# Three of seven skip products per batch summed in the states' PSUM banks, and other GpSimd costs for the planner

## Chip, cores, metric

One core of a Trainium2 chip runs the program. The metric is the device time of one execution in microseconds (us). Three runs of the kernel before took 464.29, 464.99 and 465.58 us, median 464.99.

## What is computed

Four sequences of 1024 tokens, 256 features each, float32. Four layers follow one another, each added to its input, each on a layer normalization of it: causal attention; a gated feed-forward (sigmoid gate, squared ReLU, each token mixed with its predecessor); a state-space layer; the same feed-forward again. The change is in the third, which cut to what matters is:

```python
xz = layernorm(x) @ W_in.T + b_in
x_proj, z = split(xz); z = silu(z)
B_proj = x_proj @ W_B.T * dt.mean()
x_mean = causal convolution of B_proj over time, one decay kernel per state (16 states)
y = (x_mean @ W_C.T + D_skip * x_proj) * z      # states' share + skip, gated
x = x + y @ W_out.T + b_out
```

## The kernel before

**Tiles.** A sequence ("batch" b, four of them) is two halves j = 2b and 2b+1 of 512 tokens. For the products of the third layer the normalized input lies turned, features on the partitions: xnT[j] is 128 x 2 x 512 (two blocks of 128 features). A product of one 128 x 128 weight block with one 128 x 512 data block fills one PSUM bank; in the profile it is two 128x512 matmul instructions[...]. PSUM is held as four single "banks" (pool ps_bank) and two "pairs" of banks (ps_pair).

**Seven products for eight.** The skip share of a batch is a 2 x 2 block product: output blocks (e, h), feature block e and half h. seven_products (L821) makes it with seven instead of eight products from sums of weight blocks (x_sums, weight_sums L789) and sums of data blocks (T1 to T4, stream_sums L796). Each product p1 to p7 takes a bank (unit, L826); VectorE then adds it from PSUM onto running sums (add, L834; with a bias by L840, without by L838), p1 is copied into a scratch u (ScalarE or VectorE, copies L761). The same routine makes the gates z (gates_of_batch L1680, weights wz), the queries and the second feed-forward's keys (keys_of_batch L974, tiles *_gks). skips_of_batch (L1866) calls it for the skips of batches 1 to 3; batch 0 has a plain form (skip L1841, mix_states L1920). All are generators that give one product per step, and more_gates(n) takes the next n steps of one long chain: for b = 1, 2, 3 the seven gate products of b, then the seven skip products of b.

**States' share.** mix_states_apart(b) (L1880) makes four products with contraction over 16 states only, one per quarter of TensorE's rows, which run abreast, each to a bank of its own in two pairs py (L1889). VectorE adds each to the skip block (grown, L1899), then z is multiplied by that (gated, L1903, GpSimd or VectorE). The states come by DMA (states_out, states_in L1829: tile xmT) after the convolution (L1798). Then state_outputs (L1949) multiplies with W_out (pr_pyo) and VectorE adds the result to x (L1956), and mix2.prepare normalizes it for the next layer: statistics, a power on GpSimd (L642), tiles rs_g, mrs_g, xn_g; a turn through DRAM (hT_g, L731); mixing with the predecessor (xk_g, xr_g, L927 and L930); gates r_g (L1016), values (pr_g.pv), gating (L1038), adding to x on GpSimd (L1044) and storing.

**Order of the work.** TensorE's order is written out by hand: the sequence of o.unit calls at the end of hybrid_kernel (scores, more_gates(8), mix_states(0) and so on). Each engine runs its own queue in order, so a waiting instruction holds all behind it. The orders of the other engines are made while the program is built, by the planner Order (L53). Each operation states what it needs and one or more ways, (engine, cost in us, emitter); _way (L248) takes the way that would end first by these costs. Due times are counted backwards from the products that need a result (_backwards, L131). "POOL" is GpSimd; "DVE+port" marks a VectorE operation that the planner never lets run together with GpSimd's (_start, L257). It makes 20 plans with 5 rounds each (finish, L178) and emits the one that ends first by its own costs. So a changed cost can move any operation that is planned, in all layers. A sum T or a gating z has two ways: GpSimd at 1.05, or VectorE at dve(512) = 0.62 with the port.

Of the kernel before, what the change touches and what calls it, by code (L numbers as in the profile page):

```python
# [15 lines left out]
ALU = mybir.AluOpType  # L16
# [13 lines left out]
HALF = 512  # L30
# [310 lines left out]
def dve(n):  # L341
    return 0.02 + n / 850
# [7 lines left out]
def hybrid_kernel(  # L350
# [55 lines left out]
    def pair(name):  # L406
        return ps_pair.tile([P, 2 * HALF], F32, tag="pair", name=name)
# [7 lines left out]
    def lazy(make):  # L415
        box = []

        def get():
            if not box:
                box.append(make())  # L420
            return box[0]

        return get
# [372 lines left out]
    def stream_sums(key, src, needs):  # L796

        t = [lazy(lambda k=k: cols(f"T{k}_{key}")) for k in range(KC)]

        def b(c, h):  # L800
            return src(h)[:, c, :]

        def sums(k):
            return t[(k - 1) // 2]()[:, (k - 1) % 2, :]

        for k, plus, minus in (
            (1, lambda: b(0, 1), lambda: b(0, 0)),
            (3, lambda: b(1, 1), lambda: b(0, 1)),
            (2, lambda: b(1, 1), lambda: sums(1)),
            (4, lambda: b(1, 0), lambda: sums(2)),  # L810
        ):
            def emit(engine, k=k, plus=plus, minus=minus):
                engine.tensor_sub(sums(k), plus(), minus())

            o.op(
                f"{key}.T{k}", needs + ([f"{key}.T{k - 1}"] if k in (2, 4) else []),
                ("POOL", 1.05, partial(emit, nc.gpsimd)), ("DVE+port", dve(HALF), partial(emit, nc.vector)),
            )
        return sums

# [78 lines left out]
    class Mix:  # L899
# [4 lines left out]
        def prepare(self, j, by_hand=False):  # L904

            b, h = divmod(j, 2)
            key = f"{self.tag}{j}"
            hT = self.hT[j] = lazy(lambda: cols(f"hT_{key}", HALF + 1))
            xk = self.xk[j] = lazy(lambda: cols(f"xk_{key}"))
            xr = self.xr[j] = lazy(lambda: cols(f"xr_{key}"))  # L910
            names = [f"{key}.hT{c}" for c in range(KC)]
            self.rows[j] = normalized(
                key, b, h, self.needs(j), lambda c: hT()[:, c, 1:], names, by_hand=by_hand,
                by_scalar=self.last and j < BY_SCALAR,
            )
            if h == 0:
                first = lambda: nc.gpsimd.memset(hT()[:, :, 0:1], 0.0)
                before = [f"{key}.xn0"]
            else:
                old = self.hT[j - 1]  # L920
                first = lambda: nc.gpsimd.tensor_copy(hT()[:, :, 0:1], old()[:, :, HALF:])
                before = [f"{self.tag}{j - 1}.hT{c}" for c in range(KC)] + [f"{key}.xn0"]
            o.op(f"{key}.h", before, ("POOL", 0.2, first))
            for name, t, mu, mu1 in (("xk", xk, muk, muk1), ("xr", xr, mur, mur1)):
                for c in range(KC):
                    def scale(t=t, mu=mu, c=c):
                        nc.scalar.mul(t()[:, c, :], hT()[:, c, 1:], mu[:, c : c + 1])  # L927

                    def add(t=t, mu1=mu1, c=c):
                        nc.vector.scalar_tensor_tensor(  # L930
                            t()[:, c, :], hT()[:, c, :HALF], mu1[:, c : c + 1], t()[:, c, :],
                            ALU.mult, ALU.add,
                        )

                    o.op(
                        f"{key}.{name}m{c}", [names[c], "mu1"],
                        ("ACT", act(HALF), scale),
                        delay=0.0 if name == "xk" else 0.8,
                    )
                    o.op(  # L940
                        f"{key}.{name}{c}", [f"{key}.{name}m{c}", f"{key}.h"],
                        ("DVE+port", dve(HALF) + 0.06, add),
                    )
# [77 lines left out]
        def values(self, j, g):  # L1021
            b, h = divmod(j, 2)
            key = f"{self.tag}{j}"
            r, last = self.r[j], self.last
            if last and j == 2 * NB - 1:
                for n in range(2 * g, 2 * g + 2):
                    for d0, d1 in ((0, P), (P, D)) if n == NH - 1 else ((0, D),):
                        self.last_values(j, n, d0, d1)
                return
            pv = project_rows(  # L1030
                f"{key}.pv{g}", w_fv, self.ka[j], g,
                [f"{key}.ka{c}" for c in range(KC)] + ["w_fv"],
            )
            n0 = h * NH + 2 * g

            def gate():
                rg = r()[:, ts(g, 2), :]
                nc.vector.scalar_tensor_tensor(rg, rg, 1.0, pv(), ALU.add, ALU.mult)  # L1038

            dst = out[b].rearrange("(n p) d -> p n d", p=P)  # L1040

            def add():
                xg = x[b][:, n0 : n0 + 2, :]
                nc.gpsimd.tensor_add(xg, xg, r()[:, ts(g, 2), :])  # L1044

            def store():
                nc.sync.dma_start(dst[:, n0 : n0 + 2, :], x[b][:, n0 : n0 + 2, :])

            o.op(
                f"{key}.rv{g}", [f"{key}.g{g}", f"{key}.pv{g}"], ("DVE", dve(HALF), gate),  # L1050
                frees="bank",
            )
            o.op(f"{key}.x{g}", [f"{key}.rv{g}"], ("POOL", 1.27, add))
            if last:
                o.op(None, [f"{key}.x{g}"], ("SP", 0.47, store), moves=[move(8 * P * D, 1024, True)])

# [616 lines left out]
    def sums_of_batch(b):  # L1673
        if b < NB and b not in T_of:
            T_of[b] = stream_sums(
                f"zs{b}", lambda h: xnT[2 * b + h](), columns_of(2 * b) + columns_of(2 * b + 1)
            )
        return T_of.get(b)
# [187 lines left out]
    def skips_of_batch(b):  # L1866

        there = columns_of(2 * b) + columns_of(2 * b + 1)
        src = lambda h, xb=(xnT[2 * b], xnT[2 * b + 1]): xb[h]()
        for j in (2 * b, 2 * b + 1):  # L1870
            skips[j] = lazy(lambda j=j: cols(f"skip_{j}"))
        sb = [skips[2 * b], skips[2 * b + 1]]
        sums_of_batch(b + 1)
        yield from seven_products(
            f"ss{b}", f"zs{b}", wx_block, lambda k: x_sums[:, k - 1, :], src, sums_of_batch(b),
            lambda e, h: sb[h]()[:, e, :], lambda e: b_skip[:, e : e + 1],
            ["x_sums", "b_all"], there,
        )

    def mix_states_apart(b):  # L1880

        for h in range(2):
            py[2 * b + h] = lazy(lambda h=h: pair(f"py_{2 * b + h}"))

        def emit():
            for e in range(KC):
                for h in range(2):
                    k = 2 * e + h
                    nc.tensor.matmul(  # L1889
                        py[2 * b + h]()[:, ts(e, HALF)],  # L1890
                        lhsT=w_c[k * GRP : k * GRP + S, ts(e, P)],
                        rhs=xmT[b]()[k * GRP : k * GRP + S, ts(h, HALF)],
                        start=True,
                        stop=True,
                    )

        def grown(j, e):
            t = skips[j]()[:, e, :]
            nc.vector.tensor_add(t, py[j]()[:, ts(e, HALF)], t)  # L1899

        def gated(engine, j, e):
            t = z[j]()[:, e, :]
            engine.tensor_mul(t, t, skips[j]()[:, e, :])  # L1903

        o.unit(f"pm{b}", 1.0, ["w_c", f"xmT{b}"], emit, "pair", many=2)
        for h in range(2):
            j = 2 * b + h
            for e in range(KC):
                o.op(
                    f"g{e}.{j}", [f"pm{b}", f"ss{b}.c{e + 1}{h + 1}"],  # L1910
                    ("DVE", dve(HALF) + 0.03, partial(grown, j, e)),
                    frees="pair" if e else None,
                )
                o.op(
                    f"y{e}.{j}", [f"g{e}.{j}", f"z{e}.{j}"],
                    ("POOL", 1.05, partial(gated, nc.gpsimd, j, e)),
                    ("DVE+port", dve(HALF), partial(gated, nc.vector, j, e)),
                )

# [207 lines left out]
    for b in range(NB):  # L2127
        states_in(b)
    skip(1)
    more_gates(8)  # L2130
    mix_states(0)
    more_gates(8)
    outputs(0)
    more_gates(5)
    mix_states_apart(1)
    outputs(1)
    more_gates(4)
    outputs(2)
    more_gates(4)
    mix_states_apart(2)  # L2140
    outputs(3)
    more_gates(3)
# [86 lines left out]
```

## Time and profile before

| What | Value |
|---|---|
| median of three runs | 464.99 us |
| the profiled execution | 465.0 us |
| its span, first to last instruction | 463.1 us |
| granted TensorE clock | 1.000 |
| T sums of batches: VectorE, clean (T_gks) | 0.684 us each |
| the same on GpSimd (T_gks) | 1.27 to 1.47 us each |
| gating z, GpSimd | 9 at 1.46 us |
| gating z, VectorE | 3 at 0.744 us |
| adding to x, GpSimd (L1044, second feed-forward) | 14 at 1.37 us |
| state products (L1889) | 8 instructions in 1.07 us |

How to read it: the span is cut into instructions of five engines that run side by side, each in its own order: PE (TensorE's matmuls; PEld its weight loads), DVE (VectorE), ACT (ScalarE), POOL (GpSimd), SP (issues DMAs). A row of the timeline has start, length, engine, line, operation, output<-inputs, and in brackets the idle time before and who ended it. A length holds the time in which an instruction waits inside its engine, so the same small operation can be 0.15 us in one place and 1.2 in another; and successive instructions of one engine overlap by some 0.08 us, so the distance from start to start is what a queue pays. A row of the view of waits has the waiting engine and tile, the releaser, the idle us in total, how often, and the longest.

### The profile page before, as it was taken

How to read it: one execution, taken by the hardware profiler on the slowest of the kernel's cores; microseconds unless marked ns; L12 is line 12 of the kernel's file. 1: busy time of each engine (PE TensorE's matmuls, PEld its weight loads, DVE VectorE, ACT ScalarE, POOL GpSimd, SP SyncE). 2: the span in 40 equal slices, each digit the busy share in tenths (PEclk: the TensorE clock that was granted, in tenths of full speed). 3: DMA queues.
4: the chain of work that ended last, by engine and by line, in shares of the span. 5: the costliest groups of instructions: out<-in, count | busy, mean ns of one | idle time of the engine just before them, and what ended most of it. 6: DMA issues, size and time to landing. Idle time of an engine off the chain costs nothing.

```text
span 463.1 us, 6634 instructions
## 1 busy us (share of the span) xinstructions
PE 456.0 (98%) x2052; PEld 312.5 (67%) x2052; DVE 390.2 (84%) x931; ACT 220.8 (48%) x463; POOL 143.1 (31%) x149
## 2 busy tenths in 40 slices
PE   8999999999999999999999999999999999999996
PEld 5766785667786667786777775474565758675875
DVE  3687769899969999889999977459889999999962
ACT  3422414454342433333556567441458777664652
POOL 3000102112013213121271354962052616826340
PEclk9999999999999999999999999999999999999999
DMA  8047876848455763427866989603022024252442
GB/s 242 21 127 203 250 190 168 222 132 258 117 135 139 221 194 93 118 62 237 224 177 182 275 268 271 260 17 88 11 92 91 1 86 144 81 147 99 129 144 84
DMA packets 84915, 69.44 MB, mean 150 GB/s; under 512 B 20160, under 2 KB 82576, under 8 KB 84880
## 3 DMA queue, kind: packets, MB, share of 16 engines
q1 hardware_dynamic: 84064, 68.76, 50.8%
q10 hardware_dynamic: 816, 0.26, 0.2%
q8 instruction: 16, 0.26, 0.2%
q14 instruction: 19, 0.16, 0.1%
HBM read 40.54 MB, written 28.45 MB: 149 GB/s over the span
## 4 chain that ended last, share of the span: by engine, by line
PE 86%; DVE 8%; issue 2%; DMA 1%; POOL 1%; ACT 1%; SPq 0%; DVEq 0%; POOLq 0%
PE po L1597 13%; PE sc L1492 13%; PE pv L1464 5%; PE p_zs L830 4%; PE p_ss L830 4%; PE p_qs L830 2%; PE p_gks L830 2%; PE py L1848 2%; PE pc L1798 2%; PE dust L1282 1%; DMA blocks_a<-rows_a 1%; PE pr_g0.pr L881 1%; PE pb L1735 1%; PE pp_a0.pq L774 1%; PE pr_g0.pv L881 1%
## 5 line engine op out<-in xcount | busy, mean ns | idle before, releaser
L1597 PE MATMUL po<-v,prT 128*128 128x256 f32 x288 | 67.7, 380 | 0.1
L1492 PE MATMUL sc<-xa,q 128*128 128x512 f32 (+3 forms) x192 | 67.0, 486 | 0.0
L1597 PEld LDWEIGHTS po<-v,prT 128*128 128x128 f32 x288 | 54.2, 189 | 11.6 <-issue 2.6
L1513 ACT ACTIVATE pr<-pr,nmx 128x128 f32<-128x128 f32 (+7 forms) x32 | 24.7, 773 | 64.6 <-DVE pr L1508 57.7
L1492 PEld LDWEIGHTS sc<-xa,q 128*128 128x128 f32 x192 | 35.1, 190 | 24.5 <-issue 19.6
L1464 PE MATMUL pv<-wv,xa 128*128 128x257 f32 x128 | 32.9, 380 | 0.0
L642 POOL TENSOR_TENSOR rs_a<-ve_a,minus_half 128x4 f32<-128x4 f32 x7 | 7.1, 1010 | 76.8 <-DVE ve_a L629 76.8
L1044 POOL TENSOR_TENSOR x<-x,r_f 128x512 f32<-128x512 f32 x16 | 20.3, 1271 | 33.0 <-DVE r_f L1038 32.5
L642 POOL TENSOR_TENSOR rs_h<-ve_h,minus_half 128x8 f32<-128x8 f32 x8 | 13.2, 1647 | 52.5 <-DVE ve_h L631 52.5
L1464 PEld LDWEIGHTS pv<-wv,xa 128*128 128x128 f32 x128 | 23.6, 191 | 7.8 <-issue 3.6
L1508 DVE TENSOR_SCALAR_CACHE_REDUCE pr<-sc,v 128x128 f32<-128x128 f32 (+7 forms) x32 | 26.2, 818 | 1.1
L1550 DVE STREAM_TRANSPOSE prT<-pblocks 128x384 f32<-128x384 f32 (+7 forms) x30 | 23.8, 793 | 2.4 <-DMA pblocks<-exps 2.3
L642 POOL TENSOR_TENSOR rs_f<-ve_f,minus_half 128x4 f32<-128x4 f32 x8 | 8.4, 1053 | 47.1 <-DVE ve_f L629 28.8
L1044 POOL TENSOR_TENSOR x<-x,r_g 128x512 f32<-128x512 f32 x14 | 18.9, 1371 | 11.0 <-DVE r_g L1038 11.0
L1641 POOL TENSOR_TENSOR x<-x,bout_r 128x512 f32<-128x512 f32 x16 | 20.0, 1279 | 4.5 <-ACT x L1634 4.5
L1606 DVE SCALAR_TENSOR_TENSOR x<-po,rsm,x 128x256 f32<-128x256 f32 x32 | 15.0, 470 | 4.3 <-PE po L1597 3.8
L1474 DVE TENSOR_TENSOR v<-pv,bv_r 128x257 f32<-128x257 f32 x32 | 13.4, 418 | 5.6 <-PE pv L1464 5.6
L930 DVE SCALAR_TENSOR_TENSOR xr_g<-hT_g,mur,xr_g 128x512 f32<-128x512 f32 x16 | 17.3, 1112 | 0.0
L663 ACT ACTIVATE xn_f<-x,mrs_f,rs_f 128x256 f32<-128x256 f32 x18 | 9.8, 592 | 15.5 <-DVE mrs_f L651 15.5
L1634 ACT ACTIVATE x<-x,mrs_h,rs 128x256 f32<-128x256 f32 x32 | 16.9, 592 | 0.0
L1903 POOL TENSOR_TENSOR z<-z,skip 128x512 f32<-128x512 f32 x9 | 13.1, 1462 | 10.9 <-DVE skip L1899 10.7
L663 ACT ACTIVATE xn_g<-x,mrs_g,rs_g 128x256 f32<-128x256 f32 x23 | 12.4, 589 | 8.3 <-DVE mrs_g L626 6.7
(458 smaller groups left out, 1089.8 us busy)
## 6 DMA issues: line engine op xcount, KB each, us to landing
hk<-r_dram SPq DMA_DIRECT2D x16, 512.0 KB, 9.2
rows_g<-xn_g SPq DMA_DIRECT2D x8, 512.0 KB, 2.9
blocks_g<-rows_g SPq DMA_DIRECT2D x32, 128.0 KB, 2.8
x<-in_L_attn_a_X_dram SPq DMA_DIRECT2D x7, 512.0 KB, 4.9
rows_f<-xn_f SPq DMA_DIRECT2D x7, 512.0 KB, 3.0
blocks_f<-rows_f SPq DMA_DIRECT2D x28, 128.0 KB, 2.7
rows_h<-xn_h SPq DMA_DIRECT2D x7, 512.0 KB, 3.7
blocks_h<-rows_h SPq DMA_DIRECT2D x28, 128.0 KB, 3.2
```

Source lines behind the costliest of these rows:

```text
L642: nc.gpsimd.tensor_tensor(rs()[:, :k].rearrange("p k n -> p (k n)"), ve()[:, :k].rearrange("p k n -> p (k n)"), minus_half[:, : k * NH], A ...
L663: nc.scalar.activation(place(n), split(row(n)), AF.Identity, bias=mrs()[:, k - 1, n : n + 1], scale=rs()[:, k - 1, n : n + 1],)
L830: lambda: nc.tensor.matmul(p(), lhsT=w(), rhs=data(), start=True, stop=True), "bank",
L930: nc.vector.scalar_tensor_tensor(t()[:, c, :], hT()[:, c, :HALF], mu1[:, c : c + 1], t()[:, c, :], ALU.mult, ALU.add,)
L1044: nc.gpsimd.tensor_add(xg, xg, r()[:, ts(g, 2), :])
L1464: nc.tensor.matmul(pv()[:, : D + 1], lhsT=xaj()[:, c, ts(n, P)], rhs=wv[:, c, :], start=(c == 0), stop=(c == KC - 1),)
L1492: nc.tensor.matmul(sc()[:, k * HALF : k * HALF + w], lhsT=qh()[:, c, ts(n, P)], rhs=keys[k]()[:, c, :w], start=(c == 0), stop=(c == KC - 1),)
L1508: nc.vector.tensor_scalar(dst, src, v[2 * b + h]()[:, n, D : D + 1], None, ALU.add, ALU.min, accum_out=nmx(),)
L1513: nc.scalar.activation(p()[:, :nk], p()[:, :nk], AF.Exp, bias=nmx(), scale=-1.0, accum_out=sm())
L1550: nc.vector.transpose(dst()[:, : NH * width].rearrange("p (k m a) -> p k m a", m=NH, a=GRP), blocks().rearrange("p m (k a) -> p k m a", a= ...
L1597: nc.tensor.matmul(po()[:, :D], lhsT=src()[:, ts(n, P)], rhs=v[2 * b + n // NH]()[:, n % NH, :D], start=(n == 0), stop=(n == t),)
L1641: nc.gpsimd.tensor_add(xg, xg, bout_r.unsqueeze(1).to_broadcast([P, 2, D]))
```

## The change

Two things are changed. First, for batches 1 to 3, skips_of_batch makes only p1, p6, p7 and p5 (in this order), each with a bank and VectorE adds as before; the scratch u is gone, the running sums live in the skip blocks. The other three products (p2 of block (0,0), p4 of (1,0), p3 of (0,1)) are made in mix_states_apart as the first part of the sums in the pairs py, and the state products add onto these banks (start only for the fourth, k == 3). The bias, which three adds carried, is added with the states' share (scalar_tensor_tensor in grown). The steps in more_gates are counted anew: 4 skip steps per batch instead of 7. By these counts batch 0's states (mix_states(0)) come after six products behind skip(1) instead of eight.

Second, four GpSimd costs of the planner are other numbers: sums T 1.05 to 1.45, the copy of the predecessor's column 0.2 to 0.28, adding to x 1.27 to 1.33, gating 1.05 to 1.4.

```diff
@@ -814,7 +814,7 @@
 
             o.op(
                 f"{key}.T{k}", needs + ([f"{key}.T{k - 1}"] if k in (2, 4) else []),
-                ("POOL", 1.05, partial(emit, nc.gpsimd)), ("DVE+port", dve(HALF), partial(emit, nc.vector)),
+                ("POOL", 1.45, partial(emit, nc.gpsimd)), ("DVE+port", dve(HALF), partial(emit, nc.vector)),
             )
         return sums
 
@@ -920,7 +920,7 @@
                 old = self.hT[j - 1]
                 first = lambda: nc.gpsimd.tensor_copy(hT()[:, :, 0:1], old()[:, :, HALF:])
                 before = [f"{self.tag}{j - 1}.hT{c}" for c in range(KC)] + [f"{key}.xn0"]
-            o.op(f"{key}.h", before, ("POOL", 0.2, first))
+            o.op(f"{key}.h", before, ("POOL", 0.28, first))
             for name, t, mu, mu1 in (("xk", xk, muk, muk1), ("xr", xr, mur, mur1)):
                 for c in range(KC):
                     def scale(t=t, mu=mu, c=c):
@@ -1050,7 +1050,7 @@
                 f"{key}.rv{g}", [f"{key}.g{g}", f"{key}.pv{g}"], ("DVE", dve(HALF), gate),
                 frees="bank",
             )
-            o.op(f"{key}.x{g}", [f"{key}.rv{g}"], ("POOL", 1.27, add))
+            o.op(f"{key}.x{g}", [f"{key}.rv{g}"], ("POOL", 1.33, add))
             if last:
                 o.op(None, [f"{key}.x{g}"], ("SP", 0.47, store), moves=[move(8 * P * D, 1024, True)])
 
@@ -1866,23 +1866,60 @@
     def skips_of_batch(b):
 
         there = columns_of(2 * b) + columns_of(2 * b + 1)
-        src = lambda h, xb=(xnT[2 * b], xnT[2 * b + 1]): xb[h]()
+        key = f"ss{b}"
+        T = sums_of_batch(b)
         for j in (2 * b, 2 * b + 1):
             skips[j] = lazy(lambda j=j: cols(f"skip_{j}"))
-        sb = [skips[2 * b], skips[2 * b + 1]]
         sums_of_batch(b + 1)
-        yield from seven_products(
-            f"ss{b}", f"zs{b}", wx_block, lambda k: x_sums[:, k - 1, :], src, sums_of_batch(b),
-            lambda e, h: sb[h]()[:, e, :], lambda e: b_skip[:, e : e + 1],
-            ["x_sums", "b_all"], there,
-        )
+
+        def block(e, h):
+            return lambda: skips[2 * b + h]()[:, e, :]
+
+        def unit(r, w, data, need):
+            p = lazy(lambda: bank(f"p{r}_{key}"))
+            o.unit(
+                f"{key}.p{r}", columns(HALF), ["x_sums", "b_all"] + need,
+                lambda: nc.tensor.matmul(p(), lhsT=w(), rhs=data(), start=True, stop=True), "bank",
+            )
+            return p
+
+        def add(name, r, p, more, to, need, last=True):
+            o.op(
+                f"{key}.{name}", [f"{key}.p{r}", f"{key}.{need}"],
+                ("DVE", dve(HALF) + 0.03, lambda: nc.vector.tensor_add(to(), p(), more())),
+                frees="bank" if last else None,
+            )
+
+        u1, u2, u3, u5 = block(0, 0), block(0, 1), block(1, 0), block(1, 1)
+        p = unit(1, lambda: wx_block(0, 0), lambda: xnT[2 * b]()[:, 0, :], there)
+        o.op(f"{key}.u1", [f"{key}.p1"], *copies(u1, p), frees="bank")
+        yield
+        p = unit(6, lambda: x_sums[:, 1, :], lambda: T(2), [f"zs{b}.T2"])
+        add("u2", 6, p, u1, u2, "u1")
+        yield
+        p = unit(7, lambda: x_sums[:, 2, :], lambda: T(3), [f"zs{b}.T3"])
+        add("u3", 7, p, u2, u3, "u2")
+        yield
+        p = unit(5, lambda: x_sums[:, 0, :], lambda: T(1), [f"zs{b}.T1"])
+        add("u5", 5, p, u3, u5, "u3", last=False)
+        add("u4", 5, p, u2, u2, "u3")
+        yield
 
     def mix_states_apart(b):
 
         for h in range(2):
             py[2 * b + h] = lazy(lambda h=h: pair(f"py_{2 * b + h}"))
+        T = sums_of_batch(b)
 
         def emit():
+            for h, e, w, data in (
+                (0, 0, wx_block(0, 1), xnT[2 * b]()[:, 1, :]),
+                (0, 1, wx_block(1, 1), T(4)),
+                (1, 0, x_sums[:, 3, :], xnT[2 * b + 1]()[:, 1, :]),
+            ):
+                nc.tensor.matmul(
+                    py[2 * b + h]()[:, ts(e, HALF)], lhsT=w, rhs=data, start=True, stop=False
+                )
             for e in range(KC):
                 for h in range(2):
                     k = 2 * e + h
@@ -1890,30 +1927,38 @@
                         py[2 * b + h]()[:, ts(e, HALF)],
                         lhsT=w_c[k * GRP : k * GRP + S, ts(e, P)],
                         rhs=xmT[b]()[k * GRP : k * GRP + S, ts(h, HALF)],
-                        start=True,
+                        start=(k == 3),
                         stop=True,
                     )
 
         def grown(j, e):
             t = skips[j]()[:, e, :]
-            nc.vector.tensor_add(t, py[j]()[:, ts(e, HALF)], t)
+            nc.vector.scalar_tensor_tensor(
+                t, py[j]()[:, ts(e, HALF)], b_skip[:, e : e + 1], t, ALU.add, ALU.add
+            )
 
         def gated(engine, j, e):
             t = z[j]()[:, e, :]
             engine.tensor_mul(t, t, skips[j]()[:, e, :])
 
-        o.unit(f"pm{b}", 1.0, ["w_c", f"xmT{b}"], emit, "pair", many=2)
+        there = columns_of(2 * b) + columns_of(2 * b + 1)
+        o.unit(
+            f"pm{b}", columns(HALF, 3) + 1.05,
+            ["w_c", "x_sums", "b_all", f"xmT{b}", f"zs{b}.T4"] + there, emit, "pair", many=2,
+        )
         for h in range(2):
             j = 2 * b + h
             for e in range(KC):
                 o.op(
-                    f"g{e}.{j}", [f"pm{b}", f"ss{b}.c{e + 1}{h + 1}"],
+                    f"g{e}.{j}", [f"pm{b}", f"ss{b}." + (("u1", "u4"), ("u3", "u5"))[e][h]]
+                    + ([f"ss{b}.u2"] if (e, h) == (0, 0) else [])
+                    + ([f"ss{b}.u5"] if (e, h) == (1, 0) else []),
                     ("DVE", dve(HALF) + 0.03, partial(grown, j, e)),
                     frees="pair" if e else None,
                 )
                 o.op(
                     f"y{e}.{j}", [f"g{e}.{j}", f"z{e}.{j}"],
-                    ("POOL", 1.05, partial(gated, nc.gpsimd, j, e)),
+                    ("POOL", 1.4, partial(gated, nc.gpsimd, j, e)),
                     ("DVE+port", dve(HALF), partial(gated, nc.vector, j, e)),
                 )
 
@@ -2127,16 +2172,16 @@
     for b in range(NB):
         states_in(b)
     skip(1)
-    more_gates(8)
+    more_gates(6)
     mix_states(0)
-    more_gates(8)
+    more_gates(5)
     outputs(0)
-    more_gates(5)
+    more_gates(3)
     mix_states_apart(1)
     outputs(1)
-    more_gates(4)
+    more_gates(3)
     outputs(2)
-    more_gates(4)
+    more_gates(3)
     mix_states_apart(2)
     outputs(3)
     more_gates(3)
```

## The prediction

> **What bounds the kernel now.** I read the page first, then who TensorE waited for, then the chain with the timeline where TensorE stood still, then the shares by stage. From the page:
>
> ```profile
> span 463.1 us, 6634 instructions
> PE 456.0 (98%) x2052; PEld 312.5 (67%) x2052; DVE 390.2 (84%) x931; ACT 220.8 (48%) x463; POOL 143.1 (31%) x149
> PE 86%; DVE 8%; issue 2%; DMA 1%; POOL 1%; ACT 1%; SPq 0%; DVEq 0%; POOLq 0%
> ```
>
> TensorE has an instruction in flight for 456.0 of 463.1 us. A busy matmul may be waiting unseen, so I compared start with next start: a 128x512 half takes 0.43 us nearly everywhere (the chain writes 1.72 for 4), so it really works. All its waits from the view of waits:
>
> ```profile
> PE dust L1282 <- DVE idle L427: 1.2, 1, 1.2
> PE p_gks L830 <- DVE u_gks L765: 1.0, 1, 1.0
> PE pr_g2.pr L881 <- ACT r_g L1016: 0.7, 1, 0.7
> PE pp_a0.pq L774 <- DVE xa L765: 0.3, 1, 0.3
> ```
>
> Two of the four lie behind the change, at 395 and 425 us. Start to start they cost more than their idle time: pr_g2.pr starts at 393.10, 8 matmuls of 0.216 end at 394.83, the next starts at 395.68: 0.85 lost. p_gks: 422.62 + 1.72 = 424.34, next start 425.48: 1.14 lost. Each is followed by a slow first matmul (about 0.1). Together 2.2 us. The chain shows three smaller delays: pr_g0.pr 3.72 us for 16 (elsewhere 3.45), pr_pyo0.4 1.99 for 8 (1.73), p_gks 2.83 for 6 (2.58): 0.78 more. So some 3.0 us can be had behind 310 us, and nothing more unless TensorE gets less work.
>
> Why does TensorE wait at 425? The timeline there, all engines:
>
> ```profile
> 420.85 0.68 DVE L813 TENSOR_TENSOR T_gks<-xk_g,T_gks 128x512 f32<-128x512 f32 x1
> ...
> 421.67 1.61 POOL L813 TENSOR_TENSOR T_gks<-xk_g,T_gks 128x512 f32<-128x512 f32 x1 [2.12 <-issue]
> ...
> 422.06 1.24 DVE L651 SCALAR_TENSOR_TENSOR mrs_g<-rs_g,mv_g 128x4 f32<-128x4 f32 x1
> ...
> 423.23 1.51 DVE L657 TENSOR_SCALAR xn_g<-x,mv_g,rs_g 128x256 f32<-128x256 f32 x1
> 423.28 3.81 POOL L1044 TENSOR_TENSOR x<-x,r_g 128x512 f32<-128x512 f32 x3
> ...
> 424.66 0.68 DVE L765 COPY u_gks<-p_gks 128x512 f32<-128x512 f32 x1
> ```
>
> The tiny mrs_g (0.15 us at 374.42 and 377.52) lasts until GpSimd's T_gks ends at 423.28; xn_g, 0.33 elsewhere, stands behind GpSimd's x; the copy that frees TensorE's bank is last in VectorE's queue. So VectorE is the second limit, by its own work and by GpSimd's:
>
> ```profile
> 310.00:382.80 72.80, 72.77 (x253) 42.24 (x252) 66.79 (x103) 41.19 (x124) 24.75 (x26) 1.00 0.21 63
> 382.80:421.50 38.70, 38.01 (x160) 30.16 (x161) 37.31 (x64) 24.63 (x49) 22.15 (x19) 1.00 0.37 114
> 421.50:463.10 41.60, 36.88 (x145) 26.64 (x144) 28.38 (x52) 20.42 (x35) 14.56 (x13) 1.00 0.38 121
> ```
>
> (Columns: stretch, its length, then busy us of PE, PEld, DVE, ACT, POOL, and the clock.) The clock is 1.00 throughout. VectorE is busy 37.3 of 38.7 us in the middle stretch and has room before and after it.
>
> **TensorE's part of the change: nothing.** Per batch seven products leave seven_products and come back as four in skips_of_batch and three in mix_states_apart: 7 x 0.86 both times, and four state products abreast (8 starts in 1.07 us). The granted clock is full, no weights are added.
>
> Here a rule speaks against the change. The state products now add onto banks that a full product has just written; py_3's is written by the very last matmul ahead of them. Rows: at L1925 state products already add onto product sums and take 1.07 us, as at L1889 where they start fresh; but there the last product into those banks is 6 us old. The Trainium skill, TensorEngine Tiling (Array Packing), Gotcha 1: PSUM Pressure, says that different row tiles cannot access the same bank at the same time. The four state products keep four banks, so by the row the cost is 0; if the bank behind a fresh product made them queue, it would be up to 8 x 0.43 - 1.07 = 2.4 us a batch, 7 us in all. No row shows that case. I take 0: two halves of one sum follow each other into a bank at 0.43 us throughout.
>
> **VectorE's part.** Gone per batch: two adds with bias (L840, 0.744) and one plain add (0.692), 2.18; in three batches 6.5 us. The two that stay at p5 lose their bias (0.05 each, 0.3 saved in all); twelve state adds (L1899, 0.678) become adds with bias as at L840, +0.065 each, 0.8 in all. Net -6.0 us.
>
> The order of the changed program then shows what the new GpSimd costs do: 18 operations leave GpSimd for VectorE, 13 sums T and 5 gatings z. Clean, VectorE does such a sum in 0.60 start to start (420.85 to 421.46): 18 x 0.60 = +10.8. Two relu-squares fewer (-1.3), six more normalizations xn_g of 0.33 (+2.0). VectorE thus gains about 5.5 us of clean work in spite of its nine removed adds.
>
> Against it stands the lock, whose price a row shows:
>
> ```profile
> 309.78 1.27 POOL L813 TENSOR_TENSOR T_zs<-xnT,xnT 128x512 f32<-128x512 f32 x1
> ...
> 310.01 1.59 DVE L813 TENSOR_TENSOR T_zs<-xnT,xnT 128x512 f32<-128x512 f32 x1
> ...
> 311.01 1.75 POOL L813 TENSOR_TENSOR T_zs<-xnT 128x512 f32<-128x512 f32 x1
> ...
> 311.52 1.78 DVE L813 TENSOR_TENSOR T_zs<-xnT 128x512 f32<-128x512 f32 x1
> ```
>
> The Trainium skill, SBUF — State Buffer, section SBUF: two separate sides, calls the port pair of the two engines an exclusive lock that the loser waits out, for VectorE operations with two SBUF inputs too. The row agrees (1.6 to 1.8 against 0.68). By the rule each of the 18 moved operations can itself be blocked, by one remaining GpSimd operation of about 1.3: at worst 18 x 1.9 = 34 us instead of 10.8; at best each also gives back up to 1.1 us that others stood behind it. In the tight middle stretch few moved operations meet GpSimd, so I take the clean 0.60 there.
>
> **The tight stretch, counted.** VectorE's queue from batch 3's first state add (382.81) to the sum that p6 of the third key batch needs. I price each row by its clean start-to-start (add or gate 0.60, with bias or mix 0.66, turn 0.62, statistics 0.53, small 0.1). Before: 63 instructions, 33.7 us; it ended at 421.46, so 38.65 elapsed, 4.95 of them standing still (1.1 xr_g behind z at 387.6, 1.07 mrs_g behind T_gks at 398.5, 1.1 xr_g behind x at 404.5, rest idle or small). After: 65 instructions, 35.35 us: three gatings and four sums more, some turns and mixes earlier. The first two of those stalls go with their GpSimd operations: 2.3 us; 2.65 stay. It ends at 382.8 + 35.35 + 2.65 = 420.8. Without the 0.95 lost at 395, TensorE asks for it at 421.67. It is in time by 0.9.
>
> The 395 stall goes: r_g1's last gating frees its bank near 391.4 instead of 394.3, since mixes xr_g2 stand ahead of it no more. The 425 stall goes: the copy u_gks2 is on ScalarE (0.58), T is no longer on GpSimd, and mrs_g6 stands behind the first key add. -2.2.
>
> The three small delays: x0's chain starts 4 us earlier (pyo0.0 follows batch 0's states by 5 products, earlier by 8), pr_g0 only 2.6 us earlier, so its inputs have more room; half of 0.78 goes: -0.4, bounds 0 and -0.8.
>
> **States earlier.** Batch 0's states stand behind six products instead of eight: wanted at 320.14 - 1.72 = 318.42. Their four reads are issued from 313.85, 0.64 apart, and land 2.5 to 2.8 us after issue (the view of xmT), the last at about 318.5. TensorE waits 0 to 0.3: +0.1. pyo0.0 then needs two gatings done by 323.9; in VectorE's order they stand right behind the states, near 321.0: free.
>
> **Turned columns.** T4 of batch 1 now stands on VectorE ahead of bT, while GpSimd runs x sums of 1.27: bT may be late for pbt at 293.48. Ahead of bT are 4 sums and 2 turns: slack some 0.9. 0 to 0.5: +0.3. Ahead of 288 us only the order moves, neither side proven: 0, within 0.6.
>
> Sum: -2.2 - 0.4 + 0.1 + 0.3 = -2.2; one such repaired stall usually shows a next one (VectorE has 0.9 us left, behind it mrs_g6 can be blocked by x for 1.3): +0.4. That is -1.8 on 465.0 (span 463.1 plus 1.9), which is the median of the runs too: 463.2.
>
> **Rivals.**
> - The change doesn't relieve VectorE: the planner gives it more than the adds take away, and one of the two stalls comes back elsewhere. For it: 37.2 of clean work up to the second key add against 35.4. Against: the locks that go. TensorE's work is unchanged, so 465.0 - 0.5 = 464.5, within 0.3%. Chance 0.31.
> - Slower: VectorE's queue in 382.8 to 421.5. The moved sums wait in line for xk and skip, where on GpSimd they waited alone, and every operation behind waits with them, gates that free banks included. Of VectorE's standing still, 35.35 + s beyond 38.9 (421.67 less 382.8) goes to TensorE one for one: from s = 3.5. With 1.2 us lost again at the copy behind it, the kernel is slower by 0.3% from s = 5.9 (before: 4.95); at s = 7 it loses 3.5 + 1.2 where before lost 2.2: 467.5. Chance 0.12.
> - State products queue behind a fresh bank: 3 to 7 us, less the gain: 469. Chance 0.05.
> - My forecast: 0.52.
>
> **Numbers.** A measurement tells 0.3%, 1.4 us, from no change. Faster is below 463.6: most of my case, 0.48 with a little of the first rival; slower above 466.4: 0.16; within 0.36. The range goes from all 3.0 us recovered, 462.0, to 466.3, which leaves out both slow cases.
>
> **What would show it.** Right: no wait of PE at pr_g2.pr and p_gks over 0.3 us; state products still 1.07 us; GpSimd some 18 instructions and 25 us lighter; T sums near 0.7 on VectorE; last matmul about 1.8 us earlier. Wrong: py L1926 above 1.3 us; a wait on xmT above 0.5; VectorE standing over 5 us in the middle stretch.

## The result, and the profile after

The changed kernel takes 466.55 us in the median (19 runs, 465.41 to 467.64), the kernel before 465.15 on the same chip (19 runs, 463.88 to 466.57): ratio 1.0027, 95% interval 1.0015 to 1.0038. It is slower by 0.3%, where 463.2 was forecast. Executions of one kernel differ by about 1 us to either side of the median. The profiled one took 467.52 us: its span stands 2.6 us above that of before, of which the medians show 1.4, so shifts read from the two profiles are those of two executions.

The first two rows of the page, and TensorE's three largest waits that are new (engine and tile that waited, releaser, idle us in total, how often, the longest):

```profile
span 465.7 us, 6628 instructions
PE 456.3 (98%) x2052; PEld 312.5 (67%) x2052; DVE 389.7 (84%) x940; ACT 222.5 (48%) x465; POOL 119.6 (26%) x131
```

```profile
PE pt_f7.hT L756 <- DVE xn_f L657: 1.0, 1, 1.0
PE pr_g3.pv L881 <- ACT ka_g L988: 0.9, 1, 0.9
PE pt_h7.T L756 <- ACT u_zs L764: 0.8, 1, 0.8
```

The two waits that the change was expected to repair, pr_g2.pr at 395 and p_gks at 425 us, are gone. Of the new ones, pt_f7.hT and pt_h7.T lie at 261 and 290 us, in the second layer's feed-forward and at the entry of the third layer, ahead of every instruction that the diff rewrites. I compared the start of the same matmul in both traces: within 0.25 us until 255 us, +1.74 us after the wait at 261, +2.74 after that at 290; the last matmul ends 2.15 us later (461.52 against 459.36). The rest of the difference of the spans lies in the last store, which lands 3.0 us after VectorE's last addition instead of 2.6.

Added up from start to start behind 292 us, with the slow first matmuls that follow each wait: gone are 2.2 us at 395 and 425 and all 0.78 of the three small delays. New are 1.2 at pr_g3.pv (417 us), 0.33 at 408, 0.39 at 429, 0.45 at 451 and 0.16 at batch 0's states. So the rear repaired 3.0 us and lost 2.5 again, on top of the 2.7 that it was handed.

What the front's loss looks like (the timeline; rows have start, length, engine, line, operation, output<-inputs, how often):

```profile
250.17 2.67 POOL L1641 TENSOR_TENSOR x<-x,bout_r 128x512 f32<-128x512 f32 x2 [5.83 <-ACT x L1634]
250.34 2.65 DVE L657 TENSOR_SCALAR xn_h<-x,mv_h,rs_h 128x256 f32<-128x256 f32 x2
...
257.43 0.47 DVE L1606 SCALAR_TENSOR_TENSOR x<-po,rsm,x 128x256 f32<-128x256 f32 x1
...
260.00 2.05 DVE L657 TENSOR_SCALAR xn_f<-x,mv_f,rs_f 128x256 f32<-128x256 f32 x3
261.46 0.65 PE L756 MATMUL pt_f7.hT<-ident,xn_f 128*128 128x128 f32 x3 [0.96 <-DVE xn_f L657]
...
287.24 2.49 POOL L1641 TENSOR_TENSOR x<-x,bout_r 128x512 f32<-128x512 f32 x2
287.31 1.29 DVE L651 SCALAR_TENSOR_TENSOR mrs_h<-rs_h,mv_h 128x4 f32<-128x4 f32 x2
288.53 2.41 DVE L657 TENSOR_SCALAR xn_h<-x,mv_h,rs_h 128x256 f32<-128x256 f32 x3
...
290.44 1.32 PE L756 MATMUL pt_h7.T<-ident,xn_h 128*128 128x128 f32 x8 [0.78 <-ACT u_zs L764]
```

L1641 is an addition of the third layer: the bias of its output, bout_r, is added to x beforehand on GpSimd, two tiles at a time, 16 instructions in all; nothing needs them before the outputs of the third layer are added, so the planner may put them nearly anywhere. Here two run beside xn_h, a normalization on VectorE: two tiles take 2.65 us (before, three took 1.05 at 249.94). VectorE's queue, whose order also differs from before, is then 2.2 us late: the addition from PSUM at 257.43 was at 255.22, xn_f at 260.00 was at 257.79, and TensorE needs its columns. At 287 us the same again: mrs_h takes 1.29 for two (before 0.41), xn_h 2.41 for three (before 1.05). In the trace of before, such additions ran at 232.7 and 240.4 and one alone at 285.75, over at 287.02, when xn_h began. Its rows:

```profile
249.94 1.05 DVE L657 TENSOR_SCALAR xn_h<-x,mv_h,rs_h 128x256 f32<-128x256 f32 x3
...
285.75 1.27 POOL L1641 TENSOR_TENSOR x<-x,bout_r 128x512 f32<-128x512 f32 x1
...
287.04 1.05 DVE L657 TENSOR_SCALAR xn_h<-x,mv_h,rs_h 128x256 f32<-128x256 f32 x3
```

The view puts the wait of 290 us down to ScalarE's copy u_zs, which came last for the first of these matmuls (it ended at 290.34). That copy stands behind ScalarE's own xn_h, which had waited 0.89 us for mrs_h; and the fourth matmul starts at 290.99, when VectorE's third xn_h has ended (290.93). Both ways lead back to mrs_h and xn_h.

In the rear, the new wait at 417 us:

```profile
413.74 0.61 ACT L987 ACTIVATE ka_g<-ka_g 128x512 f32<-128x512 f32 x1
414.39 0.63 ACT L988 ACTIVATE ka_g<-ka_g 128x512 f32<-128x512 f32 x1
414.92 0.71 ACT L927 ACTIVATE xr_g<-hT_g,mur 128x512 f32<-128x512 f32 x1
415.54 0.61 ACT L987 ACTIVATE ka_g<-ka_g 128x512 f32<-128x512 f32 x1
416.18 0.63 ACT L988 ACTIVATE ka_g<-ka_g 128x512 f32<-128x512 f32 x1
...
416.86 1.35 PE L881 MATMUL pr_g3.pv<-w_fv,ka_g 128*128 128x256 f32 x5 [0.94 <-ACT ka_g L988]
```

Both relu-and-squares of ka_g3 (L987, L988) stand on ScalarE, behind its scalings; before, one was on VectorE. pr_g3.pv waits for the second.

### The profile page after: what moved, and what is told of

The parts are those of the page before. It is cut to its first block, busy times and chain, and to the rows that moved or that the text cites. A ratio compares the mean times of both kernels' runs of the same rounds, so it can differ in the third digit from the quotient of the medians.

```text
span 465.7 us, 6628 instructions
## 1 busy us (share of the span) xinstructions
PE 456.3 (98%) x2052; PEld 312.5 (67%) x2052; DVE 389.7 (84%) x940; ACT 222.5 (48%) x465; POOL 119.6 (26%) x131
## 4 chain that ended last, share of the span: by engine, by line
PE 77%; DVE 12%; DMA 3%; issue 3%; SPq 1%; ACT 1%; POOL 1%; DVEq 0%; POOLq 0%; ACTq 0%
PE sc L1492 13%; PE po L1597 11%; PE pv L1464 5%; PE p_zs L830 4%; PE p_qs L830 2%; PE p_ss L1882 2%; PE py L1920 2%; DVE xk_g L930 2%; PE py L1848 2%; PE p_gks L830 2%; PE pc L1798 2%; PE dust L1282 1%; DMA blocks_a<-rows_a 1%; DMA blocks_g<-rows_g 1%; DVE T_gks L813 1%
## 5 line engine op out<-in xcount | busy, mean ns | idle before, releaser
L1641 POOL TENSOR_TENSOR x<-x,bout_r 128x512 f32<-128x512 f32 x16 | 20.8, 1313 | 23.1 <-ACT x L1634 23.1
L1044 POOL TENSOR_TENSOR x<-x,r_g 128x512 f32<-128x512 f32 x14 | 20.2, 1459 | 20.5 <-DVE r_g L1038 20.4
L642 POOL TENSOR_TENSOR rs_h<-ve_h,minus_half 128x8 f32<-128x8 f32 x8 | 13.2, 1645 | 26.5 <-DVE ve_h L631 19.9
L642 POOL TENSOR_TENSOR rs_g<-ve_g,minus_half 128x4 f32<-128x4 f32 x8 | 9.0, 1122 | 37.9 <-DVE ve_g L621 27.2
L663 ACT ACTIVATE xn_f<-x,mrs_f,rs_f 128x256 f32<-128x256 f32 x20 | 10.8, 590 | 14.2 <-DVE mrs_f L651 14.2
L927 ACT ACTIVATE xk_g<-hT_g,muk 128x512 f32<-128x512 f32 x16 | 11.0, 714 | 10.9 <-DVE hT_g L731 10.7
L927 ACT ACTIVATE xk_f<-hT_f,muk 128x512 f32<-128x512 f32 x16 | 10.9, 715 | 10.7 <-DVE hT_f L731 10.2
```

The costliest lines, as they stand in the source:

```text
L642: nc.gpsimd.tensor_tensor(rs()[:, :k].rearrange("p k n -> p (k n)"), ve()[:, :k].rearrange("p k n -> p (k n)"), minus_half[:, : k * NH], A ...
L1641: nc.gpsimd.tensor_add(xg, xg, bout_r.unsqueeze(1).to_broadcast([P, 2, D]))
```

## Experiments

**Theory A:** the front lost 2.7 us because the new costs and counts made the planner order work otherwise that the change doesn't touch; the rear by itself gains. **Theory B:** the rear is bound by VectorE, which got the T sums and gatings z; what the front loses would be waited for there anyway.

To keep one stretch's order while changing another, I had each build write down its planner's order (every unit and operation with the engine chosen) and gave the kernel that list in place of its planner:

```diff
+def _scripted(self):
+    for n, way in SCRIPT:                  # number in the planner's log, engine
+        e = self.log[n]
+        if e["kind"] == "unit":
+            e["emit"]()
+        else:
+            [w for w in e["ways"] if w[0] == way][0][2]()
+Order.finish = _scripted
```

"Front" is everything ahead of the first changed product (ss1.p2 or ss1.p6, some 315 us): 1442 entries before and 1444 after. Both kernels hand their planner the same operations there; the two more are additions of bout_r, which the kernel before issues later. "Rear" is the rest.

**One part alone: the share with the old costs.**

```diff
-                ("POOL", 1.45, ...)      # T; likewise 0.28, 1.33, 1.4
+                ("POOL", 1.05, ...)      #            0.2,  1.27, 1.05
```

> The changed kernel with GpSimd's old costs (1.05, 0.2, 1.27, 1.05) in the planner; the products are those of the changed kernel. Its order ahead of 292 us is a third one, and in it two adds of bout_r still follow h7's rs on GpSimd, so they meet h7's normalization again, while none stands in front of h6's. Theory A (the loss lies in the order ahead of 292 us): one of the two front stalls comes back, +1.2 us of +2.6, and the end stands near 465.2, ratio to before 0.999 to 1.001. Theory B (the loss is VectorE's T and z multiplies, which the new costs moved over to it): with ten T and eight z multiplies on GpSimd again the loss goes, 464.3 or less, ratio 0.998 or lower, whatever the front does.

468.76 us, ratio 1.008 (1.0061 to 1.0098). Both theories missed: it is slower than the kernel before and than the changed one.

**The other part alone: the new costs with the old products** (the same four numbers, in the kernel before).

> The kernel before with only the four new costs of GpSimd in the planner; no product is changed. Seven T and five z multiplies on GpSimd instead of fifteen and nine. Theory A: front order is again another, with two adds of bout_r right behind h7's rs: +1.2 there, and the stalls of 395 and 425 us stay as they are or move a little: 466.2, ratio 1.001 to 1.004. Theory B: all of VectorE's added 7 us without the relief of the adds that the products took over: 467.5 or more, ratio 1.005 or more.

471.83 us, ratio 1.0145 (1.0121 to 1.0168): far over A's number, over B's too. So each part alone costs 3.5 and 6.6 us, and together they cost 1.4. The fronts of these two kernels are orders of their own, so where it is lost can't be read from the totals; the next runs separate front and rear.

**Front of before, rear of the changed kernel, and the reverse.**

```diff
-    SCRIPT = front of after + rear of after
+    SCRIPT = front of before + rear of after     # first run
+    SCRIPT = front of after + rear of before     # second run, products of before
```

> The changed kernel, in which everything ahead of the first changed product of layer 3 (some 315 us) is issued in the order of the kernel before, step by step and each on its engine of before; from there on in the changed kernel's own order. Theory A: the two stalls at 261 and 290 us go, 2.6 us come off, less what the rear can't take: 463.9, ratio to before 0.996 to 0.9985. Theory B: the rear is bound by VectorE and would only wait longer: no better than 466, ratio 1.001 to 1.003.

464.15 us, ratio 0.9977 (0.9968 to 0.9986): A's number, and a kernel faster than both. Its waits show it: of the three new ones of the changed kernel, the two of the front are gone and the rear's is left.

```profile
PE pr_g3.pv L881 <- ACT ka_g L988: 0.9, 1, 0.9
```

> The kernel before, in which everything ahead of the first changed product (some 315 us) is issued in the changed kernel's order, and the rest in its own; products and adds are those of before. Theory A: the two front stalls come in, and nothing else changes: +2.6, less what the stalls of 395 and 425 us may take up (up to 1): 467.2, ratio 1.003 to 1.006. Theory B: the front's order is of no account: 465.2, ratio 0.999 to 1.001.

467.75 us, ratio 1.0066 (1.0042 to 1.009), a little over A's range and far from B's. The changed front costs 0.66% with the old rear and 0.50% (1.0027 less 0.9977) with the new: 3.1 and 2.3 us. Theory B's claim that the front is of no account falls.

**The four additions of bout_r.** Which part of the front's order is it? The changed kernel, with h3's two additions (250 us) and h6's two (287 us) issued behind h7's normalization, then with h6's alone:

```diff
 # GpSimd's queue
-... rs_h4, h3.o0, h3.o1, rs_f7 ... h7.rs, h6.o0, h6.o1, h5.o0 ...
+... rs_h4, rs_f7 ... h7.rs, h3.o0, h3.o1, h6.o0, h6.o1, h5.o0 ...
```

> The changed kernel, in which four adds of bout_r on GpSimd, two for h3 (at 250 us) and two for h6 (at 287 us), are issued behind h7's normalization (some 292 us) and nothing else is moved. Theory A1 (these adds hold VectorE's normalizations while PE waits for them): the first stall (261 us, 1.3 to 1.7) falls to some 0.3, because VectorE is still later there by two transposes; the second (290 us, 1.0) goes; the four adds at 292 us and after cost nothing: 464.2, ratio to before 0.997 to 0.999. Theory A2 (it is the order of the transposes and of the adds from PSUM on VectorE that matters, and the lock only happens to stand beside it): the stalls stay at over half, 465.5 or more.

467.92 us, ratio 1.0053 (1.0033 to 1.0073). The first stall went wholly (the matmul behind it 2.23 us earlier than in the changed kernel, 0.63 of which this execution was ahead before), the second grew to three waits, 2.5 us of idle time. My edit was at fault: "behind h7's normalization" in the list orders nothing between two engines. GpSimd reached the four additions right behind h7.rs, and they stood where two had stood:

```profile
285.01 5.03 POOL L1641 TENSOR_TENSOR x<-x,bout_r 128x512 f32<-128x512 f32 x4
285.08 1.29 DVE L651 SCALAR_TENSOR_TENSOR mrs_h<-rs_h,mv_h 128x4 f32<-128x4 f32 x2 [0.35 <-POOL rs_h L642]
286.30 4.31 DVE L657 TENSOR_SCALAR xn_h<-x,mv_h,rs_h 128x256 f32<-128x256 f32 x3
```

Beside four additions xn_h takes 4.31 for three, beside two 2.41, beside none 1.05. That is a dose and its effect, and it speaks for A1, although the time missed both theories.

Part of that time is not the additions' alone: right behind the three waits the granted clock is 0.50 from 291.99 to 295.41 us, and TensorE falls back another 1.6 us against the changed kernel (groups of pb matmuls start up to 0.86 us apart instead of 0.43). Of the six executions, the four with a mean clock of 0.995 or 0.996, the profiled one among them, took 467.9 to 468.9 us, the two with 0.998 took 466.0 and 466.5, about the time of the changed kernel. Why the clock drops in some executions and not in others is not shown.

> The same with only h6's two adds (at 287 us) behind h7's normalization. Theory A1: only the second stall goes, 1.0 to 1.2 of the 2.6: 465.5, ratio to before 0.9995 to 1.0015. Theory A2: no change from the changed kernel, 466.5.

466.73 us, ratio 1.0037 (1.0024 to 1.0051). For the same reason this kernel's GpSimd queue is that of the changed kernel; it repeats its time and tells nothing of A2.

**The same four additions, late in time too.** h5.o0 waits until ScalarE has grown its x (298 us in the changed kernel), so what is queued behind it is held back. First I put the four behind h7.o1 and the T sum that follows:

```diff
-... h7.rs, h6.o0, h6.o1, h5.o0, h7.o0, h5.o1, h7.o1, zs3.T2, g0.me ...
+... h7.rs, h5.o0, h7.o0, h5.o1, h7.o1, zs3.T2, h6.o0, h6.o1, h3.o0, h3.o1, g0.me ...
```

> The changed kernel, in which the same four adds of bout_r on GpSimd (h3's two, h6's two) stand in GpSimd's queue behind zs3's T sum, which comes at some 303 us behind an add that ScalarE releases at 298, so that in time too none of them meets h7's normalization. Theory A1 (the adds hold the normalizations): both front stalls go, 2.2 to 2.7 us; the four adds at 304 to 309 us stand beside VectorE's work where the kernel before has six: 464.2, ratio to before 0.9965 to 0.9995. Theory A2 (the order of VectorE's own queue makes the stalls): 465.5 or more.

465.72 us, ratio 1.0016 (1.0007 to 1.0025). The time is the one that A2 gave, but not for A2's reason: both front stalls went (2.92 us at 288), and 1.8 was lost again at 340 us. I had expected that T sum at 303; it came at 327, and the additions behind it stood in front of layer 3's first statistics (ms_g, which was at 329.67 in the run with the front of before):

```profile
327.26 1.60 POOL L813 TENSOR_TENSOR T_zs<-xnT,T_zs 128x512 f32<-128x512 f32 x1 [27.19 <-issue]
328.83 5.39 POOL L1641 TENSOR_TENSOR x<-x,bout_r 128x512 f32<-128x512 f32 x4
334.20 0.22 POOL L612 TENSOR_SCALAR ms_g<-ms_g 128x4 f32<-128x4 f32 x1
...
339.73 1.13 PE L830 MATMUL p_zs<-xnT,w_in 128*128 128x512 f32 x2 [0.80 <-DVE x L2001]
```

So they went directly behind h7.o1, ahead of that T sum:

```diff
+... h7.rs, h5.o0, h7.o0, h5.o1, h7.o1, h6.o0, h6.o1, h3.o0, h3.o1, zs3.T2, g0.me ...
```

> As the run with the four adds of bout_r at 304 us (465.72 us), but ahead of zs3's T sum in GpSimd's queue, right behind h7's own two adds, so that they run at some 300 to 305 us. In the run before, that T sum came at 327 us, the four adds ran from 329 to 334 in front of layer 3's first statistics on GpSimd, and the products of 340 us waited 1.5 us for VectorE. If that is all that stood against the moved adds: no wait at 261, 290 or 340 us, 464.0, ratio to before 0.997 to 0.9995, level with the run that has the whole front of before (464.15). If the front of before has other merits than the place of the four adds: 465.5 again.

463.49 us, ratio 0.996 (0.9947 to 0.9972), a little under the forecast. The changed kernel with four instructions of GpSimd in another place, none of them one that the diff rewrites, is faster than before by 0.4%. With the row of eight additions from 295.14 us on (the four moved ones at 300.06 to 303.77), mrs_h and xn_h have their lengths again:

```profile
285.58 0.24 DVE L651 SCALAR_TENSOR_TENSOR mrs_h<-rs_h,mv_h 128x4 f32<-128x4 f32 x2 [0.52 <-POOL rs_h L642]
285.74 1.06 DVE L657 TENSOR_SCALAR xn_h<-x,mv_h,rs_h 128x256 f32<-128x256 f32 x3
...
295.14 2.50 POOL L1641 TENSOR_TENSOR x<-x,bout_r 128x512 f32<-128x512 f32 x2 [9.17 <-ACT x L1634]
```

In this trace VectorE, ScalarE and TensorE issue instruction for instruction what they issue in the changed kernel; GpSimd alone has another order. The addition from PSUM that came at 257.43 there is at 255.23 here, and neither front wait is left. So A2, the order of VectorE's own queue, falls, and A1 is shown.

**What the rear does with the two parts.** With the same front of before, the rear of the share alone and of the costs alone (lists joined as above):

> The kernel of the share alone (GpSimd's old costs, 468.76 us), with everything ahead of the first changed product issued in the order of before. It tells what the new costs do for the rear when the front is the same: the share's rear with the old costs. If front and rear add up: its front lost 2.2 against before's, so 466.6, ratio 1.002 to 1.004, and the new costs are worth 2.4 us in the rear. If the costs matter only by what they do to the front: 464.2, ratio 0.997 to 0.999.

468.28 us, ratio 1.0063 (1.0047 to 1.0079): a miss by 1.7. The share's rear with the old costs loses by itself.

> The kernel of the costs alone (the products of before, 471.83 us), with everything ahead of the first product of layer 3 that the share changes issued in the order of before. With the runs of the same front (before 465.0, share alone 468.3, both 464.15) it completes a table of the rear. If the costs move T and z multiplies to a VectorE that has no room for them unless the products take over its adds: still well above before, 468.5, ratio 1.006 to 1.009. If costs and share add up in the rear (share alone +3.1, both -1.0, so costs alone -4): 461, ratio 0.991.

468.75 us, ratio 1.0083 (1.0063 to 1.0103), as the first of the two readings had it. So the fronts that the share alone and the costs alone had of their own (468.76 and 471.83 us) cost some 0.2% and 0.6% more than the front of before.

| rear, all with the front of before | us | ratio |
|---|---|---|
| as before | 464.8 to 465.25 | 1 |
| share, old costs | 468.28 | 1.0063 |
| old products, new costs | 468.75 | 1.0083 |
| share and new costs | 464.15 | 0.9977 |

The two don't add up: together they are 1.7% better than the sum of the two losses. In the stretch 382.8 to 421.5 us, busy time (length, PE, PEld, DVE, ACT, POOL, clock) of the share with the old costs, then with the new ones:

```profile
382.80:421.50 38.70, 37.92 (x159) 29.71 (x158) 38.32 (x63) 20.06 (x34) 20.35 (x17) 1.00 0.32 102
```

```profile
382.80:421.50 38.70, 37.73 (x158) 29.55 (x157) 37.91 (x66) 21.65 (x39) 13.03 (x11) 1.00 0.35 112
```

VectorE is full in both (38.3 and 37.9 of 38.7); GpSimd holds 20.4 us beside it in the first, where TensorE waits 4.0 us behind 310 us (for VectorE 2.5, GpSimd 0.8, ScalarE 0.7), and 13.0 in the second, where it waits 0.9. Only the 0.8 for GpSimd lie in this stretch, though; the other waits are at 356 us and from 423 to 452. With the costs alone GpSimd is as light (13.2), but VectorE still has the adds that the share takes away, and TensorE waits 2.1 us for a key sum (ka_g) and 1.4 for a gating. That trace is of its slowest execution (471.48 us), in which the clock is at 0.50 too, from 431.9 to 435.3 us, right behind the wait of 2.1; the run of the costs with their own front has both waits and no such drop. That these two loads are the cause, and not the order that comes with each, is argued from these rows and not shown: each rear is another plan.

**The wait at 417 us.** In the run with the front of before, the second relu-and-square of g3 goes to VectorE:

```diff
-g3.ka1 on ScalarE, behind g5.xrm0
+g3.ka1 on VectorE, behind gks1.c22 (the add that makes its data)
```

> As the run with the front of before and the rear of the changed kernel (464.15 us), and in it one relu and square of g3 (its second block) on VectorE, right behind the add that makes its data, instead of on ScalarE. If the stall of 0.93 us at 414 us is ScalarE's queue: it goes, and about 0.9 comes off, 463.2, ratio to before 0.995 to 0.9965. If VectorE's own queue is as tight there, the stall comes back within 15 us at a product that waits for VectorE, and nothing comes off: 464.1.

465.27 us, ratio 1.0 (0.9988 to 1.0012): worse than without, by intervals that barely part. The wait at 414 went and others came in the rear, all behind VectorE:

```profile
PE p_gks L830 <- DVE ka_g L838: 1.3, 1, 1.3
PE pp_g7.pk L774 <- DVE xk_g L930: 0.8, 1, 0.8
PE p_gks L830 <- DVE T_gks L813: 0.5, 1, 0.5
```

One instruction more in VectorE's queue at 409 us, and TensorE waits for VectorE at 422, 427 and 450 us. Theory B is right about the place: in this run VectorE has no room behind 405 us. (The same trace has a wait of 1.0 us at 288 in the front, which the run with the same front doesn't have. This execution came there 1.3 us earlier than that one, and VectorE's transposes waited until 285.56 for their DMA, as they did there until 285.44; so it lost its lead, not more. Behind 427 us it is 0.9 us later, behind 450 1.9.) Left on ScalarE but moved ahead of one scaling:

```diff
-... g3.ka0, g5.xrm0, g3.ka1 ...
+... g3.ka0, g3.ka1, g5.xrm0 ...
```

> As the run with the front of before and the rear of the changed kernel (464.15 us); on ScalarE alone the last relu and square of g3 is issued ahead of one scaling (xr of g5) instead of behind it. VectorE's queue is untouched. If ScalarE's order makes the stall of 0.93 us at 414: 0.6 of it goes (the scaling's row), 463.6, ratio to before 0.995 to 0.998. If the rear is bound by VectorE from 405 us on, what is gained at 414 is waited for again at the products of 422 to 448 us that wait for VectorE: 464.1.

463.78 us, ratio 0.9979 (0.9966 to 0.9991). By the profile 0.6 us came off at 414 and went again at 426, where p_gks now waits 0.7 for VectorE's ka_g; by the ratios nothing can be told from 0.9977.

> The same, and the last relu and square of g3 ahead of one scaling on ScalarE, which took 0.4 us off the run with the front of before (464.15 to 463.78). The two edits stand 100 us apart; if they add up: 463.6, ratio to before 0.996 to 0.9985, the changed kernel with five instructions in other places.

463.69 us, ratio 0.9961 (0.9947 to 0.9975), the changed kernel with both repairs: no better than with the additions alone (0.996).

## Why the prediction was wrong

The step that failed is "Ahead of 288 us only the order moves, neither side proven: 0, within 0.6." It was +2.7 us in the profiled execution (1.7 at 261 us, 1.0 at 290, a stretch where only the turned columns had been priced) and 2.3 by the runs. Of the 3.2 us between the forecast of 1.8 faster and the measured 1.4 slower, that is the greater part; the rest lies in the rear, below. I had priced GpSimd's lock in the rear from its row and not asked where the new order put GpSimd's 2.5 us pairs in the front. The order was there to read: h6's two additions directly behind h7's rs, on whose output mrs_h and xn_h wait. With the row I had (mrs_g 1.24 instead of 0.15 beside GpSimd's T), some 2 us for such a meeting (two operations held for 1.1 each, an estimate) could have been written down. The planner does count the port, and still put them there; why is open.

The other steps:

- **TensorE's part, nothing:** right. State products took 1.07 us in each of the three batches, on banks that a full product had just written. The rule weighed there (the Trainium skill, TensorEngine Tiling (Array Packing), Gotcha 1: PSUM Pressure) costs nothing in this case, and that rival is out.
- **VectorE's part, +5.5 of clean work:** the page bears it out only in so far as VectorE is not relieved (389.7 us busy, before 390.2). GpSimd is 18 instructions and 23.5 us lighter (predicted 18 and 25), T sums on VectorE take 0.68. So VectorE's moved work would be paid for by waits behind GpSimd that went; that is argued from these sums, not counted row by row. (The sum counts four additions a batch that carried the bias, and so has the kernel; the description of the change says three.) The Trainium skill, SBUF — State Buffer, section SBUF: two separate sides, says that the loser waits the lock out; xn_h at 1.05, 2.41 and 4.31 us for three beside no, two and four additions agrees.
- **The tight stretch, -2.2:** right (though the two stalls taken off add up to 2.2 and not 2.3), both stalls went, and TensorE no longer waits at the stretch's end for the T sum. So the slow rival (VectorE's queue in this stretch) is not what made the kernel slower, though it is the nearest to what happened in the rear: the run with one instruction more in that queue waits there at once.
- **The small delays, -0.4 (bound -0.8):** all 0.78 went. **States earlier, +0.1:** 0.16. **Turned columns, +0.3:** 0, the shift stays at 2.7 from 291 to 321 us.
- **The next stall, +0.4:** mis-sized, the second step that failed: the right kind and too small, 2.4 in four places, half of it ScalarE's queue at 417 us. I had watched VectorE there.

With the front repaired, the kernel is faster than before by 1.1 us (front of before, ratio 0.9977) and 1.9 us (four additions moved, ratio 0.996), where 1.8 was predicted. In the changed kernel's own profile the rear repaired 3.0 where I took 2.6, and lost 2.5 where I took 0.8: 0.5 gained instead of 1.8. That 1.9 stands next to 1.8 is therefore no proof of the sum.

## What to carry to other kernels

Where a planner makes the order, a change of its costs or counts is a change to the whole kernel: compare the orders everywhere, and price each long operation of one engine that newly stands beside a short, awaited one of the engine it shares a port with. A part measured alone tells little when the parts share a full engine: here each alone lost 0.6 to 0.8% with the same front, each under a plan of its own, and both together gained. Moving an instruction in a list moved it in time here only where it came to stand behind something that waits.

## What was not expected of the hardware

The two engines nearly take turns. In the run with four additions at 285 us they end at 286.28, 287.50, 288.78 and 290.05; the three xn_h beside them start at 286.30, 287.58 and 288.85 and last 1.36, 1.35 and 1.75 instead of 0.40 each. The first two end some 0.15 us behind the second and the third addition. The last one sits through the fourth addition and a memset of GpSimd (L1762) that follows it, and ends 0.15 us behind that, so the turns are not strict. A row of GpSimd's additions thus doesn't cost its neighbour one wait but, in these rows, one per instruction for as long as the row lasts. In this way four additions, 5 us of work on an engine that is busy for 26% of the span, decide 0.7% of the kernel's time by their place (1.0027 against 0.996).
